# A pair-product kernel: W in one buffer, chunks aligned at their ends, one buffer for the transposed x

## The chip, the cores, the metric

The kernel runs on one core of a Trainium2 chip. The metric is the device time of one execution in microseconds; a quoted time is the median of a kernel's fast runs. TensorE (PE) does the matmuls, VectorE (DVE) the multiplications, ScalarE (ACT) copies out of PSUM and issues loads, SyncE (SP) issues the stores and W's loads, and 16 DMA engines move the data.

## The reference

For every row b of x (4096 rows, 32 fields of 64 numbers) and every pair of fields i < j, the output is `(x[b, i] @ W[pair]) * x[b, j]`, with one 64 x 64 matrix for each of the 496 pairs:

```python
i_idx, j_idx = np.triu_indices(32, k=1)
vdotw = einsum('bpd,pde->bpe', x[:, i_idx, :], W)   # x: 4096 x 32 x 64, W: 496 x 64 x 64
out = (vdotw * x[:, j_idx, :]).reshape(4096, -1)    # 4096 x 31744 float32 = 520 MB
```

## The kernel before

There are 32 tiles of 128 rows. Field i needs one matrix product whose right side is (31 - i) * 64 columns wide: all its matrices side by side. Two neighbouring fields make a "pair" p = 0 to 15 (fields 2p and 2p + 1); the even one uses partitions 0 to 63 of PE, the odd one 64 to 127. The odd field has 64 columns less. Pairs are cut in chunks of at most 512 columns a field. PE writes a chunk of both fields to two PSUM banks, and one DVE instruction multiplies both with x into an output ring in SBUF. Four stores a tile empty the ring.

```python
STORES = [[0, 1], [2, 3], [4, 5, 6], [7, 8, 9, 10, 11, 12, 13, 14, 15]]   # pairs of each store
PREFETCH_AT = [5, 6]
RING = 28160                                       # columns; a tile makes 31744
...
for p in range(NPR):                               # W: sixteen buffers, sixteen loads
    wp = const.tile([P, width[2 * p]], F32, tag=f"w{p}", name=f"w{p}")
    nc.sync.dma_start(out=wp, in_=w[:, woff[p] : woff[p] + width[2 * p]])
...
if t + 1 < NT and p in PREFETCH_AT:                # the next tile's x, transposed into a second buffer
    ...
    transpose_x(xTs[t + 1], t + 1, xs[t + 1], PREFETCH_AT.index(p))
for c0 in range(0, width[2 * p], CHUNK):           # chunks counted from the fields' starts
    n = [max(0, min(CHUNK, width[2 * p + h] - c0)) for h in range(2)]
    ...                                            # one matmul a field
    o = [off[2 * p + h] - o0 + c0 for h in range(2)]
    xj = [(2 * p + h + 1) * D + c0 for h in range(2)]
    if n[1] > half - BANK and o[1] + n[0] <= store_w[s]:
        nc.vector.tensor_tensor(                   # both fields, n[0] columns each
            runs(osb, o[0], o[1], n[0]), runs(pm, 0, half, n[0]),
            runs(xt, xj[0], xj[1], n[0]), ALU.mult)
    else:
        ...                                        # one instruction a field
nc.sync.dma_start(out=out[ts(t, P), o0 : o0 + store_w[s]], in_=osb)
```

In the last chunk of a pair the odd field has 64 columns less, but the joint instruction writes n[0] columns for both, so it writes 64 columns of rubbish past the odd field's end, where the next pair begins. The next pair's first instruction overwrites them.

Of the kernel before, what the change touches and what calls it, by code (L numbers as in the profile page):

```python
# [1 line left out]

# [6 lines left out]

F32 = mybir.dt.float32  # L10
ALU = mybir.AluOpType

P = 128
BANK = 512
BANKS = 8
CHUNK = BANK

STORES = [[0, 1], [2, 3], [4, 5, 6], [7, 8, 9, 10, 11, 12, 13, 14, 15]]
PREFETCH_AT = [5, 6]
RING = 28160  # L20


@with_exitstack
def pair_bilinear_kernel(
    ctx: ExitStack,
    tc: tile.TileContext,
    x: bass.AP,
    w: bass.AP,
    out: bass.AP,
    F: int,  # L30
    D: int,
):




















    nc = tc.nc
    B = x.shape[0]
    NT = B // P
    NPR = F // 2

    width = [(F - 1 - i) * D for i in range(F)]
    off = [sum(width[:i]) for i in range(F)]
    woff = [sum(width[0 : 2 * p : 2]) for p in range(NPR)]  # L60
    store_w = [sum(width[2 * p] + width[2 * p + 1] for p in g) for g in STORES]

    const = ctx.enter_context(tc.tile_pool(name="const", bufs=1))
    xtpool = ctx.enter_context(tc.tile_pool(name="xT", bufs=2))
    psum = ctx.enter_context(tc.tile_pool(name="ps", bufs=1, space=bass.MemoryType.PSUM))

    ident = const.tile([P, P], F32, tag="ident", name="ident")
    make_identity(nc, ident)

    def runs(tl, a, b, n):  # L70

        ap = tl[:, a : a + n]
        return bass.AP(ap.tensor, ap.offset, [list(ap.ap[0]), [b - a, 2], list(ap.ap[1])])


    xbuf = [const.tile([P, (F + 1) * D], F32, tag=f"x{b}", name=f"x{b}") for b in range(2)]
    for xb in xbuf:
        nc.gpsimd.memset(xb[:, F * D :], 0.0)  # L78

    def load_x(t):  # L80
        xt = xbuf[t % 2]
        nc.scalar.dma_start(out=xt[:, : F * D], in_=x[ts(t, P), :])
        return xt

    pring = psum.tile([P, BANKS * BANK], F32, tag="pring", name="pring")
    bank = 0

    def take_banks(n):

        nonlocal bank  # L90
        if bank + n > BANKS:
            bank = 0
        got = pring[:, bank * BANK : (bank + n) * BANK]
        bank = (bank + n) % BANKS
        return got

    def transpose_x(xT, t, xt, g):

        n = 2 * BANK // P
        pt = take_banks(2)  # L100
        for c in range(n):
            nc.tensor.transpose(pt[:, ts(c, P)], xt[:, ts(n * g + c, P)], ident)  # L102
        nc.scalar.copy(xT[:, ts(g, 2 * BANK)], pt)  # L103

    def new_xT(t):
        return xtpool.tile([P, NPR * P], F32, tag="xT", name=f"xT_{t}")

    ring = const.tile([P, RING], F32, tag="ring", name="ring")
    at = 0
    xs = {0: load_x(0)}  # L110

    w_sb = []
    for p in range(NPR):
        wp = const.tile([P, width[2 * p]], F32, tag=f"w{p}", name=f"w{p}")
        nc.sync.dma_start(out=wp, in_=w[:, woff[p] : woff[p] + width[2 * p]])
        w_sb.append(wp)

    xTs = {0: new_xT(0)}
    for g in range(2):
        transpose_x(xTs[0], 0, xs[0], g)  # L120

    for t in range(NT):
        xt, xT = xs.pop(t), xTs.pop(t)
        if t + 1 < NT:
            xs[t + 1] = load_x(t + 1)
        for s, group in enumerate(STORES):
            if at + store_w[s] > RING:
                at = 0
            osb = ring[:, at : at + store_w[s]]
            at += store_w[s]  # L130
            o0 = off[2 * group[0]]
            for p in group:
                if t + 1 < NT and p in PREFETCH_AT:
                    if t + 1 not in xTs:
                        xTs[t + 1] = new_xT(t + 1)
                    transpose_x(xTs[t + 1], t + 1, xs[t + 1], PREFETCH_AT.index(p))
                for c0 in range(0, width[2 * p], CHUNK):
                    n = [max(0, min(CHUNK, width[2 * p + h] - c0)) for h in range(2)]
                    half = -(-n[0] // BANK) * BANK
                    pm = take_banks(2 * half // BANK)  # L140
                    for b0 in range(0, n[0], BANK):
                        b1 = min(b0 + BANK, n[0])
                        for h in range(2):
                            if b0 < n[h]:
                                nc.tensor.matmul(  # L145
                                    pm[:, h * half + b0 : h * half + b1],
                                    xT[h * D : (h + 1) * D, ts(p, P)],
                                    w_sb[p][h * D : (h + 1) * D, c0 + b0 : c0 + b1],
                                    start=True,
                                    stop=True,  # L150
                                )
                    o = [off[2 * p + h] - o0 + c0 for h in range(2)]
                    xj = [(2 * p + h + 1) * D + c0 for h in range(2)]
                    if n[1] > half - BANK and o[1] + n[0] <= store_w[s]:
                        nc.vector.tensor_tensor(  # L155
                            runs(osb, o[0], o[1], n[0]),
                            runs(pm, 0, half, n[0]),
                            runs(xt, xj[0], xj[1], n[0]),
                            ALU.mult,
                        )  # L160
                    else:
                        for h in range(2):
                            if n[h]:
                                nc.vector.tensor_tensor(  # L164
                                    osb[:, o[h] : o[h] + n[h]],
                                    pm[:, h * half : h * half + n[h]],
                                    xt[:, xj[h] : xj[h] + n[h]],
                                    ALU.mult,
                                )
            nc.sync.dma_start(out=out[ts(t, P), o0 : o0 + store_w[s]], in_=osb)  # L170


# [33 lines left out]
```

## Time and profile before

| | before |
|---|---|
| time | 1337.95 us (1337.75 to 1338.13, 6 runs) |
| bytes moved | 562.9 MB: 520.1 written, 41.9 read, the rest instructions |
| busy: PE, DVE, ACT | 86%, 90%, 5% of the span |
| DMA engines | at nine tenths or more in 39 of 40 slices |
| DVE waits for stores | 68 us in 35 waits |

### The profile page before, as it was taken

The page shows a single profiled execution, that of the slowest core. Times are in us where ns is not written, and L with a number is a line of the kernel's source. Part 1 is how long each engine was busy: PE and PEld are TensorE (multiplying, and loading weights), DVE is VectorE, ACT ScalarE, POOL GpSimd, SP SyncE. Part 2 cuts the span into 40 slices and gives each one's busy share as a digit, 9 for nine tenths or more (in the row PEclk, how much of TensorE's full clock was granted, in tenths as well). Part 3 has the DMA queues.
Part 4 walks back from the last instruction along what each step waited for, and adds up shares of the span by engine and source line. Part 5 has one row for each costly group of instructions (what it writes and reads, how often), then busy time and mean ns, then how long its engine had stood idle before and what let it go on. Part 6 is the DMA issues. An engine that isn't in the chain of part 4 may idle for free. (4 is left out here: it accounts for less than half of the span.)

```text
span 1335.8 us, 13084 instructions
## 1 busy us (share of the span) xinstructions
PE 1154.1 (86%) x5376; PEld 529.9 (40%) x5376; DVE 1199.1 (90%) x1344; ACT 66.1 (5%) x65; POOL 0.9 (0%) x8
## 2 busy tenths in 40 slices
PE   7898898988888889898888898898988888888883
PEld 3343343433343444344334444343443333333331
DVE  5999898999899999899999899989988989999994
ACT  1000000000000000000000000000000000000000
POOL 0000000000000000000000000000000000000000
PEclk9999999899999999999999999999999999999997
DMA  9999999999999999999999999999999999999998
GB/s 392 435 426 431 436 408 434 415 426 431 419 417 425 428 429 416 418 424 420 424 436 419 418 421 426 424 426 421 418 430 414 426 423 413 424 427 430 418 420 370
DMA packets 25403, 562.88 MB, mean 421 GB/s; under 512 B 2944, under 2 KB 3328, under 8 KB 4864
## 3 DMA queue, kind: packets, MB, share of 16 engines
q1 hardware_dynamic: 20736, 528.49, 92.6%
q10 hardware_dynamic: 4608, 33.56, 6.0%
q8 instruction: 42, 0.69, 0.2%
q14 instruction: 17, 0.14, 0.0%
HBM read 41.94 MB, written 520.09 MB: 421 GB/s over the span
## 5 line engine op out<-in xcount | busy, mean ns | idle before, releaser
L155 DVE TENSOR_TENSOR ring<-pring,x 128x1024 f32<-128x1024 f32 (+3 forms) x1088 | 1154.2, 1107 | 116.9 <-DMA out_dram<-ring 68.0
L145 PE MATMUL pring<-w,xT 64*128 64x512 f32 (+4 forms) x4864 | 1087.8, 563 | 132.3 <-DVE ring L155 127.9
L145 PEld LDWEIGHTS pring<-w,xT 64*128 64x128 f32 x4864 | 472.9, 192 | 721.4 <-DVE ring L155 611.7
L103 ACT COPY xT<-pring 128x1024 f32<-128x1024 f32 x64 | 64.8, 1012 | 1197.1 <-PE pring L102 1197.1
L102 PE MATMUL pring<-ident,x 128*128 128x128 f32 x512 | 71.5, 285 | 30.7 <-DMA x<-in_x_dram 30.3
L102 PEld LDWEIGHTS pring<-ident,x 128*128 128x128 f32 x512 | 57.0, 144 | 65.6 <-issue 65.6
L164 DVE TENSOR_TENSOR ring<-pring,x 128x64 f32<-128x64 f32 (+4 forms) x256 | 70.9, 297 | 3.3
L103 ACT ACT_TABLE_LOAD x1 | 1.3, 1283 | 1.7 <-PEq L198 1.7
masks.py:199 POOL TENSOR_SCALAR_AFFINE_SELECT ident<-ident 128x128 f32<-128x128 f32 x1 | 0.3, 292 | 0.0
L78 POOL MEMSET x<- 128x64 f32 x2 | 0.2, 152 | 0.0
masks.py:197 POOL MEMSET ident<- 128x128 f32 x1 | 0.2, 204 | 0.3 <-POOLq L198 0.3
L198 POOL MEMSET const-bfloat16-1.0<- 128x1 bf16 x1 | 0.1, 101 | 0.0
L198 POOL MEMSET const-uint8-127<- 128x1 uint8 x1 | 0.1, 101 | 0.0
L198 POOL MEMSET const-float32-0.0<- 128x1 f32 x1 | 0.1, 98 | 0.2 <-issue 0.2
L198 POOL MEMSET const-float32-1.0<- 128x1 f32 x1 | 0.1, 98 | 0.0
## 6 DMA issues: line engine op xcount, KB each, us to landing
out_dram<-ring SPq DMA_DIRECT2D x32, 4896.0 KB, 18.6
out_dram<-ring SPq DMA_DIRECT2D x32, 3936.0 KB, 17.4
out_dram<-ring SPq DMA_DIRECT2D x32, 3776.0 KB, 19.0
out_dram<-ring SPq DMA_DIRECT2D x32, 3264.0 KB, 19.4
x<-in_x_dram ACTq DMA_DIRECT2D x32, 1024.0 KB, 17.8
w<-in_w_dram SPq DMA_DIRECT2D x1, 992.0 KB, 7.5
w<-in_w_dram SPq DMA_DIRECT2D x1, 928.0 KB, 11.8
w<-in_w_dram SPq DMA_DIRECT2D x1, 864.0 KB, 13.4
```

The source lines that it names most:

```text
L78: nc.gpsimd.memset(xb[:, F * D :], 0.0)
L102: nc.tensor.transpose(pt[:, ts(c, P)], xt[:, ts(n * g + c, P)], ident)
L103: nc.scalar.copy(xT[:, ts(g, 2 * BANK)], pt)
L145: nc.tensor.matmul(pm[:, h * half + b0 : h * half + b1], xT[h * D : (h + 1) * D, ts(p, P)], w_sb[p][h * D : (h + 1) * D, c0 + b0 : c0 + b1 ...
L155: nc.vector.tensor_tensor(runs(osb, o[0], o[1], n[0]), runs(pm, 0, half, n[0]), runs(xt, xj[0], xj[1], n[0]), ALU.mult,)
L164: nc.vector.tensor_tensor(osb[:, o[h] : o[h] + n[h]], pm[:, h * half : h * half + n[h]], xt[:, xj[h] : xj[h] + n[h]], ALU.mult,)
L198: nc = bacc.Bacc("TRN2", target_bir_lowering=False, num_devices=1)
```

## The change

The intent was less of everything: five loads of W instead of sixteen, one buffer for the transposed x instead of two, no padding of x. The chunks are now counted from the fields' ends. There both fields of a pair reach the same x columns, so one instruction can take the same columns of x for both (a step of 0), and the 64 overhanging columns fall in front of the odd field, on the end of the even one.

```diff
-PREFETCH_AT = [5, 6]
+LOADS = [[0], [1], [2, 3], [4, 5, 6], [7, 8, 9, 10, 11, 12, 13, 14, 15]]
+FIRST_HALF_AT, SECOND_HALF_AT = 9, 3
...
+    xT = const.tile([P, NPR * P], F32, tag="xT", name="xT")
...
+    w_sb = const.tile([P, sum(width[0::2])], F32, tag="w", name="w")
+    done = 0
+    for g in LOADS:
+        upto = woff[2 * g[-1]] + width[2 * g[-1]]
+        nc.sync.dma_start(out=w_sb[:, done:upto], in_=w[:, done:upto])
+        done = upto
...
+                if p == SECOND_HALF_AT:
+                    transpose_x(xt, 1)
+                if p == FIRST_HALF_AT and t + 1 < NT:
+                    transpose_x(xbuf[(t + 1) % 2], 0)
+                first = (width[2 * p] - 1) % BANK + 1
+                for c1 in range(first, width[2 * p] + 1, BANK):
+                    n = first if c1 == first else BANK
+                    c0 = c1 - n
...
+                    xj = xt[:, (2 * p + 1) * D + c0 : (2 * p + 1) * D + c1]
+                    o = [off[2 * p + h] - o0 + c0 - h * D for h in range(2)]
+                    if odd and (c0 or c1 < width[2 * p]):
                         nc.vector.tensor_tensor(
-                            runs(osb, o[0], o[1], n[0]),
-                            runs(pm, 0, half, n[0]),
-                            runs(xt, xj[0], xj[1], n[0]),
+                            runs(osb, o[0], o[1], n),
+                            runs(pm, 0, BANK, n),
+                            bass.AP(xj.tensor, xj.offset, [xj.ap[0], [0, 2], xj.ap[1]]),
                             ALU.mult,
                         )
```

The ring keeps its size, though 8 KB a partition of SBUF come free.

More of the change, by code (lines that the diff above doesn't have):

```diff
@@ L15 @@
 BANKS = 8
-CHUNK = BANK
 STORES = [[0, 1], [2, 3], [4, 5, 6], [7, 8, 9, 10, 11, 12, 13, 14, 15]]
-PREFETCH_AT = [5, 6]
+LOADS = [[0], [1], [2, 3], [4, 5, 6], [7, 8, 9, 10, 11, 12, 13, 14, 15]]
+FIRST_HALF_AT, SECOND_HALF_AT = 9, 3
 RING = 28160
@@ L53, in pair_bilinear_kernel @@
     nc = tc.nc
-    B = x.shape[0]
-    NT = B // P
+    NT = x.shape[0] // P
     NPR = F // 2
@@ L59, in pair_bilinear_kernel @@
     off = [sum(width[:i]) for i in range(F)]
-    woff = [sum(width[0 : 2 * p : 2]) for p in range(NPR)]
+    woff = [i % 2 * D + sum(width[i % 2 : i : 2]) for i in range(F)]
     store_w = [sum(width[2 * p] + width[2 * p + 1] for p in g) for g in STORES]
     const = ctx.enter_context(tc.tile_pool(name="const", bufs=1))
-    xtpool = ctx.enter_context(tc.tile_pool(name="xT", bufs=2))
     psum = ctx.enter_context(tc.tile_pool(name="ps", bufs=1, space=bass.MemoryType.PSUM))
@@ L73, in runs @@
         return bass.AP(ap.tensor, ap.offset, [list(ap.ap[0]), [b - a, 2], list(ap.ap[1])])
-    xbuf = [const.tile([P, (F + 1) * D], F32, tag=f"x{b}", name=f"x{b}") for b in range(2)]
-    for xb in xbuf:
-        nc.gpsimd.memset(xb[:, F * D :], 0.0)
+    xbuf = [const.tile([P, F * D], F32, tag=f"x{b}", name=f"x{b}") for b in range(2)]
     def load_x(t):
-        xt = xbuf[t % 2]
-        nc.scalar.dma_start(out=xt[:, : F * D], in_=x[ts(t, P), :])
-        return xt
+        nc.scalar.dma_start(out=xbuf[t % 2], in_=x[ts(t, P), :])
     pring = psum.tile([P, BANKS * BANK], F32, tag="pring", name="pring")
@@ L95, in take_banks, with transpose_x @@
         return got
-    def transpose_x(xT, t, xt, g):
+    xT = const.tile([P, NPR * P], F32, tag="xT", name="xT")
+    def transpose_x(xt, g):
         n = 2 * BANK // P
@@ L103, in transpose_x @@
         nc.scalar.copy(xT[:, ts(g, 2 * BANK)], pt)
-    def new_xT(t):
-        return xtpool.tile([P, NPR * P], F32, tag="xT", name=f"xT_{t}")
     ring = const.tile([P, RING], F32, tag="ring", name="ring")
     at = 0
-    xs = {0: load_x(0)}
-    w_sb = []
-    for p in range(NPR):
-        wp = const.tile([P, width[2 * p]], F32, tag=f"w{p}", name=f"w{p}")
-        nc.sync.dma_start(out=wp, in_=w[:, woff[p] : woff[p] + width[2 * p]])
-        w_sb.append(wp)
-    xTs = {0: new_xT(0)}
-    for g in range(2):
-        transpose_x(xTs[0], 0, xs[0], g)
+    load_x(0)
+    w_sb = const.tile([P, sum(width[0::2])], F32, tag="w", name="w")
[4 more added lines that the diff above has]
+        done = upto
+    transpose_x(xbuf[0], 0)
     for t in range(NT):
-        xt, xT = xs.pop(t), xTs.pop(t)
+        xt = xbuf[t % 2]
         if t + 1 < NT:
-            xs[t + 1] = load_x(t + 1)
+            load_x(t + 1)
         for s, group in enumerate(STORES):
@@ L132, in pair_bilinear_kernel @@
             for p in group:
-                if t + 1 < NT and p in PREFETCH_AT:
-                    if t + 1 not in xTs:
-                        xTs[t + 1] = new_xT(t + 1)
-                    transpose_x(xTs[t + 1], t + 1, xs[t + 1], PREFETCH_AT.index(p))
-                for c0 in range(0, width[2 * p], CHUNK):
-                    n = [max(0, min(CHUNK, width[2 * p + h] - c0)) for h in range(2)]
-                    half = -(-n[0] // BANK) * BANK
-                    pm = take_banks(2 * half // BANK)
-                    for b0 in range(0, n[0], BANK):
-                        b1 = min(b0 + BANK, n[0])
-                        for h in range(2):
-                            if b0 < n[h]:
-                                nc.tensor.matmul(
-                                    pm[:, h * half + b0 : h * half + b1],
-                                    xT[h * D : (h + 1) * D, ts(p, P)],
-                                    w_sb[p][h * D : (h + 1) * D, c0 + b0 : c0 + b1],
-                                    start=True,
-                                    stop=True,
-                                )
-                    o = [off[2 * p + h] - o0 + c0 for h in range(2)]
-                    xj = [(2 * p + h + 1) * D + c0 for h in range(2)]
-                    if n[1] > half - BANK and o[1] + n[0] <= store_w[s]:
@@ new lines, in pair_bilinear_kernel @@
+                if p == SECOND_HALF_AT:
[6 more added lines that the diff above has]
+                    c0 = c1 - n
+                    odd = width[2 * p + 1] and c1 > D
+                    pm = take_banks(2)
+                    for h in range(1 + bool(odd)):
+                        a = woff[2 * p + h] + c0 - h * D
+                        nc.tensor.matmul(
+                            pm[:, h * BANK : h * BANK + n],
+                            xT[h * D : (h + 1) * D, ts(p, P)],
+                            w_sb[h * D : (h + 1) * D, a : a + n],
+                            start=True,
+                            stop=True,
+                        )
+                    xj = xt[:, (2 * p + 1) * D + c0 : (2 * p + 1) * D + c1]
+                    o = [off[2 * p + h] - o0 + c0 - h * D for h in range(2)]
+                    if odd and (c0 or c1 < width[2 * p]):
@@ L161, in pair_bilinear_kernel @@
                     else:
-                        for h in range(2):
-                            if n[h]:
-                                nc.vector.tensor_tensor(
-                                    osb[:, o[h] : o[h] + n[h]],
-                                    pm[:, h * half : h * half + n[h]],
-                                    xt[:, xj[h] : xj[h] + n[h]],
-                                    ALU.mult,
-                                )
+                        for h in range(1 + bool(odd)):
+                            nc.vector.tensor_tensor(
+                                osb[:, o[h] + h * D : o[h] + n],
+                                pm[:, h * (BANK + D) : h * BANK + n],
+                                xj[:, h * D :],
+                                ALU.mult,
+                            )
             nc.sync.dma_start(out=out[ts(t, P), o0 : o0 + store_w[s]], in_=osb)
@@ L185 @@
     first = [sum(n[:i]) for i in range(F)]
-    halves = [
-        np.concatenate(
-            [
-                np.pad(wt[:, first[i] : first[i] + n[i]], ((0, 0), (0, h), (0, 0)))
-                for i in range(h, F, 2)
-            ],
-            axis=1,
-        )
-        for h in range(2)
-    ]
-    w = np.ascontiguousarray(np.stack(halves)).reshape(2 * D, -1)
+    w = np.zeros((2, D, sum(n[0::2]), D), wt.dtype)
+    for h in range(2):
+        of_h = [wt[:, first[i] : first[i] + n[i]] for i in range(h, F, 2)]
+        w[h, :, h : h + sum(n[h::2])] = np.concatenate(of_h, axis=1)
+    w = w.reshape(2 * D, -1)
     nc = bacc.Bacc("TRN2", target_bir_lowering=False, num_devices=1)
```

## The prediction

> **What bounds the kernel now.** I read the page first: the engines' totals, the slices, the DMA queues.
>
> ```profile
> span 1335.8 us, 13084 instructions
> ...
> PE 1154.1 (86%) x5376; PEld 529.9 (40%) x5376; DVE 1199.1 (90%) x1344; ACT 66.1 (5%) x65; POOL 0.9 (0%) x8
> ...
> DVE  5999898999899999899999899989988989999994
> ...
> DMA  9999999999999999999999999999999999999998
> GB/s 392 435 426 431 436 408 434 415 426 431 419 417 425 428 429 416 418 424 420 424 436 419 418 421 426 424 426 421 418 430 414 426 423 413 424 427 430 418 420 370
> ...
> q1 hardware_dynamic: 20736, 528.49, 92.6%
> q10 hardware_dynamic: 4608, 33.56, 6.0%
> ```
>
> DVE is 90% busy and PE 86%, but the DMA row is at nine tenths in every slice from the first to the last but one. The kernel writes 520 MB, which the change cannot shrink, and reads 42 MB. The chain of waits is of little use: it goes back only 3% of the span, all on DVE. So I asked who waits for whom:
>
> ```profile
> DVE ring L155 <- DMA out_dram<-ring: 68.0, 35, 3.0
> ...
> PE pring L102 <- DMA x<-in_x_dram: 30.3, 23, 8.5
> DVE ring L155 <- PE pring L145: 16.7, 7, 13.6
> ```
>
> The columns are total us, number of waits, the longest one. DVE waits 68 us for stores to clear the output ring, about once for each of the 32 tiles of 128 rows, and waits for PE hardly at all after its 13.6 us start. A ring full of stores means the stores are behind, not DVE. The timeline of DVE shows one such cycle (start, duration, what, and in brackets the idle time before it):
>
> ```profile
> 479.53 9.00 DVE L155 TENSOR_TENSOR ring<-pring,x 128x1024 f32<-128x1024 f32 x8 [2.44 <-DMA out_dram<-ring]
> ...
> 501.52 0.23 DVE L164 TENSOR_TENSOR ring<-pring,x 128x64 f32<-128x64 f32 x1
> 501.66 8.07 DVE L155 TENSOR_TENSOR ring<-pring,x 128x1024 f32<-128x1024 f32 x7
> ...
> 520.44 9.00 DVE L155 TENSOR_TENSOR ring<-pring,x 128x1024 f32<-128x1024 f32 x8 [2.40 <-DMA out_dram<-ring]
> ```
>
> A tile takes 520.44 - 479.53 = 40.9 us. DVE waits 2.4 us of it, at pair 4, for the previous tile's last and largest store; then it computes pairs 4 to 15 until 501.75 (501.52 + 0.23), when that tile's last store is issued. The median issue-to-landing time of these stores is 18.6 us, and 18.6 + 22.2 = 40.8: the loop closes. That alone would say that DVE's 22.2 us matter one for one. The packet records of the trace say otherwise. I sorted them onto 16 engines by letting each packet start where another ended. On 15 engines a 30,208-byte packet takes 1.119 us; on one it takes 1.149 us on average, and the 26,112- and 31,488-byte packets are also some 2% slower there. Summed over the kernel, that one engine is busy 1330.6 us of 1335.8, with 1.5 us of gaps after its first packet at 1.8 us and its last byte 1.3 us before the end. The other 15 are busy about 1312 us and idle about 17. Near 502 us the fifteen run dry for 0.6 us, until the new last store reaches them at 502.6; the slow one still has work until 505.6. Hence the bound: **one DMA engine that never stops**. DVE may be about 3 us later per tile, or any amount earlier, and the slow engine does not notice.
>
> **What the Trainium skill says.** "DMA: Bandwidth & Descriptors", section "Bandwidth", gives a fabric ceiling of 435 GB/s for the 16 engines together; the trace agrees: 421 GB/s over the whole span, up to 436 in a slice. 562.88 MB at 435 would be 1294 us, so no rearrangement of compute gets below that, 3.3% under today. The same page, "Latency and other measured facts", says that two of the 16 engines are usually slower in traces and suspects a descriptor ring that only GpSimd-issued DMAs have. The trace shows one slow engine with all DMAs issued from SP and ACT, so it agrees with the observation and not with that reason. "VectorE: DVE Perf Modes", section "The perf-mode tier table", has a two-tensor fp32 instruction with an operand in PSUM at one element a cycle, with no mode to gain or lose. The trace agrees: the 128x1024 multiply took 1217 ns and the 128x896 one 1079 ns, 1.08 ns per element between them (a cycle at the page's 0.96 GHz is 1.04 ns). I therefore expect nothing from x being read once for both fields: each field still streams its elements, merely from an address that repeats.
>
> **The change part by part.**
> (1) W in one buffer. W is the same 8.39 MB in five loads instead of 16. Its packets are one row each, and their durations lie on a line: 256 bytes 18 ns, 7,424 bytes 281 ns, so 0.0367 ns a byte plus about 8.6 ns a packet. Eleven fewer loads are 88 fewer packets on each engine (8 rows each): 88 x 8.6 ns = 0.76 us, plus 88/8 = 11 semaphore writes of 9 ns = 0.1 us. This lies on the bounding engine and at the front, where it shifts all that follows: -0.9 us. W now lands in coarser steps, which could starve PE: the loads finish at about 27.6 us whatever the cuts, and pair 7, the first of the last load, is reached near 38 us by the timeline. Pairs 2 and 3 (one load, done by an estimate of some 17 us from bytes at 424 GB/s) are reached at about 21 us. No wait.
> (2) Start. Only 8 of 16 transposes come before the first matmul. The timeline has PE transposing from 8.54 to 12.19 us and its first multiplying matmul at 12.12; the first copy of x's transpose ended at 11.53. So DVE starts 0.5 to 0.6 us sooner, and the first store would be issued at about 24.1 instead of 24.68. But the DMA engines are full of W until 27.6 us: worth nothing.
> (3) Chunk ends aligned. The matmul count is unchanged (4864 + 512), by the built program. DVE goes from 42 to 43 instructions a tile: pairs 1 and 6 become one instruction each instead of two, pairs 12 to 14 become two each instead of one.
>
> ```profile
> L155 DVE TENSOR_TENSOR ring<-pring,x 128x1024 f32<-128x1024 f32 x768 | 903.2, 1217 | 110.0 <-DMA out_dram<-ring 68.0 <-PE pring L145 16.7 <-PE pring L102 2.5
> ...
> L155 DVE TENSOR_TENSOR ring<-pring,x 128x896 f32<-128x896 f32 x128 | 138.1, 1079 | 0.0
> ...
> L155 DVE TENSOR_TENSOR ring<-pring,x 128x640 f32<-128x640 f32 x96 | 78.5, 818 | 3.7 <-DVE ring L155 0.5
> ...
> L155 DVE TENSOR_TENSOR ring<-pring,x 128x384 f32<-128x384 f32 x96 | 52.8, 550 | 3.2
> ...
> L164 DVE TENSOR_TENSOR ring<-pring,x 128x320 f32<-128x320 f32 x32 | 15.3, 480 | 0.0
> L164 DVE TENSOR_TENSOR ring<-pring,x 128x256 f32<-128x256 f32 x32 | 13.2, 411 | 0.0
> L164 DVE TENSOR_TENSOR ring<-pring,x 128x192 f32<-128x192 f32 x32 | 11.1, 347 | 0.0
> L164 DVE TENSOR_TENSOR ring<-pring,x 128x128 f32<-128x128 f32 x32 | 8.9, 279 | 0.0
> ```
>
> (Columns: count, then busy us, then mean ns of one.) Split forms grow by 67 ns per 64 elements, so 384 and 448 columns should cost about 547 and 614. Pair 1: 818 - (480 + 411) = -73. Pair 6: 550 - (347 + 279) = -76. Pairs 12 to 14: (614 + 547 + 480 + 411 + 347 + 279) - (1079 + 818 + 550) = +231. Sum +82 ns a tile, 2.6 us over 32; on the stretch from pair 4 to 15 it is +155 ns. Both are far inside the 3 us of slack: worth nothing. The overhanging columns that are computed and overwritten go from 10 to 9 a tile, in the same instructions' sizes as counted above.
> (4) One transposed-x buffer. Half of the transposes move to pair 9 of the tile before and half to pair 3. The 30.3 us that PE waits for x, 8.5 of it at the start and the rest at pair 5, because x lands near 521 us in the tile shown, vanish at pair 9, some 11 us later. DVE has three chunks buffered in PSUM then, and its wait for the transposes was 2.5 us in all. The overwritten half has long been read by PE, which is in order. Worth nothing. The freed SBUF is not given to the ring, which would be the only use of it that touches the DMA.
>
> Sum: -0.9 us. 1337.8 - 0.9 = 1336.9 us.
>
> **The rivals.**
> (a) DVE is the bound after all, through the loop 18.6 + 22.2. For it: the sum closes, and the fifteen engines' 0.6 us gap. Then +155 ns x 31 tiles = +4.8 us, 1342 us; or, if reading x twice from one place made DVE faster, up to 0.6 x 31 = 18 us less, 1319 us, where the fifteen engines would be full. Against it: the slow engine's 1.5 us of gaps in 1335.8.
> (b) The repeating read makes DVE slower. DVE has about 40.9 - 2.4 = 38.5 us of work a tile, so above 6% it would replace the DMA as the bound; 10% would give 42.4 us a tile, +1.5 x 31 = 46 us, 1384 us. Nothing in the trace speaks for it: joint reads with strides already run at the same rate as flat ones.
> (c) New waits of PE at pairs 3 and 9, or on the coarse W loads, stall DVE. A stall under 3 us a tile is hidden behind the slow engine; one at the start is hidden up to the 27.6 us at which W is done. 1337 us.
> (d) Another chip, with another slow engine or none. Without one, the fifteen's time would rule: about 1320 us for both kernels, no difference between them.
>
> **Range and chances.** The bytes are fixed and the bounding resource is full, so the spread is that of executions (0.3 us here) and of rival (a)'s small side, +5 or a few us less: 1331 to 1342. Faster by over 2% means below 1311, which needs the slow engine to lose 26 us of work: 0.01. Slower by over 2% needs rival (b): 0.02. Within 2%: 0.97.
>
> **What would show it.** DMA share again about 1 in all slices; the slow engine again without gaps; the tile period again 40.9 us; DVE's wait for stores still 60 to 75 us; W's packets about 19.6 us on an engine instead of 20.5; PE's wait for x about 8 us, all at the start; DVE's 128x1024 multiply at about 1217 ns. I am wrong if DVE's mean there rises by over 6%, if its waits for stores vanish, or if the period moves by more than 0.2 us.

## The result, and the profile after

| | before | after |
|---|---|---|
| time | 1337.95 us | 1338.02 us (1337.91 to 1338.11, 6 runs) |
| DVE waits for stores / for PE | 68.0 / 19.2 us | 101.6 / 22.8 us |
| PE waits for x | 30.3 us | 8.7 us |

The ratio is 1.0001 (95% interval 0.9988 to 1.0013). A ratio is the mean time of one kernel's fast runs over that of the other's of the same rounds, so not quite the ratio of the medians quoted. The change does nothing to the time.

The page of the kernel after (totals, slices, DMA queues; q1 carries W and the stores, q10 carries x):

```profile
span 1336.3 us, 13134 instructions
...
PE 1164.7 (87%) x5376; PEld 552.9 (41%) x5376; DVE 1183.0 (89%) x1376; ACT 66.1 (5%) x65; POOL 0.7 (0%) x6
...
DMA  9999999999999999999999999999999999999998
...
q1 hardware_dynamic: 19152, 528.49, 92.6%
q10 hardware_dynamic: 4608, 33.56, 6.0%
```

The DMA row and the bytes are as before; only the packets of q1 are fewer, 19,152 for 20,736. DVE has 32 instructions more and yet is 16 us less busy. Who waits for whom, after (total us, number, longest):

```profile
DVE ring L154 <- DMA out_dram<-ring: 101.6, 40, 4.1
DVE ring L154 <- PE pring L144: 22.8, 16, 13.6
...
PE pring L105 <- DMA x<-in_x_dram: 8.7, 1, 8.7
```

DVE waits 34 us longer for the stores: it became faster, and all of that turned into waiting. Of PE's waits for x only the first one, at the start, is left. The landing of the largest store (last column, median us from issue to landing), before and after:

```profile
out_dram<-ring SPq DMA_DIRECT2D x32, 4896.0 KB, 18.6
```

```profile
out_dram<-ring SPq DMA_DIRECT2D x32, 4896.0 KB, 19.5
```

It got longer as DVE's part got shorter. Since DVE waits for this landing in about every tile, landing and DVE's work roughly add up to the period whichever of them sets it. So "the sum closes" was no evidence for the prediction's rival (a). The timeline of DVE after, for the same tile as in the prediction:

```profile
479.66 6.81 DVE L154 TENSOR_TENSOR ring<-pring,x 128x896 f32<-128x896 f32 x7 [3.75 <-DMA out_dram<-ring]
...
499.12 2.40 DVE L162 TENSOR_TENSOR ring<-pring,x 128x448 f32<-128x448 f32 x7
501.44 12.46 DVE L154 TENSOR_TENSOR ring<-pring,x 128x896 f32<-128x896 f32 x12
...
520.61 6.81 DVE L154 TENSOR_TENSOR ring<-pring,x 128x896 f32<-128x896 f32 x7 [3.12 <-DMA out_dram<-ring]
```

The period is 520.61 - 479.66 = 40.95 us, as before. What changed is the wait at pair 4: 3.1 to 3.8 us in the tiles shown, instead of 2.4.

I sorted the trace's packet records onto 16 engines again (each packet starts where another ended, and each engine takes 8 packets of each store). The sorting can swap neighbours that end at the same time, but the engine that lags stands apart:

| run (its profiled execution, us) | span | slow engine busy | its gaps | the other fifteen busy |
|---|---|---|---|---|
| before | 1335.8 | 1330.6 | 1.5 | 1309 to 1316 |
| after | 1336.3 | 1331.5 | 1.1 | 1309 to 1315 |

A second, separate sorting gives the slow engine 1332.1 and 1332.5 us busy with 0.6 and 0.4 us of gaps, so these figures are good to about 2 us. It finds one slow engine of the 16 in the traces of all kernels here: about 1.00 us (median) for a packet of 26,112 bytes, where the others take 0.97.

### The profile page after: what moved, and what is told of

Its sections match the earlier page's. It is cut to its first block, busy times and chain, and to the rows that moved or that the text cites. A ratio compares the mean times of both kernels' runs of the same rounds, so it can differ in the third digit from the quotient of the medians.

```text
span 1336.3 us, 13134 instructions
## 1 busy us (share of the span) xinstructions
PE 1164.7 (87%) x5376; PEld 552.9 (41%) x5376; DVE 1183.0 (89%) x1376; ACT 66.1 (5%) x65; POOL 0.7 (0%) x6
## 3 DMA queue, kind: packets, MB, share of 16 engines
q1 hardware_dynamic: 19152, 528.49, 92.6%
## 4 chain that ended last, share of the span: by engine, by line
DMA 45%; DVE 36%; PE 9%; issue 8%; DVEq 0%; ACT 0%
DMA out_dram<-ring 45%; DVE ring L154 30%; PE pring L144 9%; DVE ring L162 5%; DMA x<-in_x_dram 1%; DVEq L154 0%; PE pring L105 0%; ACT xT L106 0%; DVEq L193 0%
## 5 line engine op out<-in xcount | busy, mean ns | idle before, releaser
L144 PE MATMUL pring<-w,xT 64*128 64x512 f32 (+4 forms) x4864 | 1102.6, 568 | 143.3 <-DVE ring L154 131.8
L154 DVE TENSOR_TENSOR ring<-pring,x 128x1024 f32<-128x1024 f32 (+3 forms) x1056 | 1104.6, 1107 | 135.3 <-DMA out_dram<-ring 101.6
L144 PEld LDWEIGHTS pring<-w,xT 64*128 64x128 f32 x4864 | 497.3, 194 | 706.5 <-DVE ring L154 508.4
L162 DVE TENSOR_TENSOR ring<-pring,x 128x64 f32<-128x64 f32 (+3 forms) x320 | 97.6, 355 | 0.3
## 6 DMA issues: line engine op xcount, KB each, us to landing
x<-in_x_dram ACTq DMA_DIRECT2D x32, 1024.0 KB, 18.1
```

What stands on the lines that cost most here:

```text
L144: nc.tensor.matmul(pm[:, h * BANK : h * BANK + n], xT[h * D : (h + 1) * D, ts(p, P)], w_sb[h * D : (h + 1) * D, a : a + n], start=True, st ...
L154: nc.vector.tensor_tensor(runs(osb, o[0], o[1], n), runs(pm, 0, BANK, n), bass.AP(xj.tensor, xj.offset, [xj.ap[0], [0, 2], xj.ap[1]]), ALU ...
L162: nc.vector.tensor_tensor(osb[:, o[h] + h * D : o[h] + n], pm[:, h * (BANK + D) : h * BANK + n], xj[:, h * D :], ALU.mult,)
```

## The experiments

Twelve kernels ran, in four calls, each on another chip (4, 5, 10 and 6); the kernel before ran in each call and took 1337.6 to 1338.0 us. Theory A is the prediction's: one DMA engine without gaps sets the time. Theory B, its rival, is the loop of a store's landing (18.6 us) and DVE's work behind it (22.2 us).

**DVE slower on purpose.** Two, then four of the 1024-wide multiplies are done twice, always behind the wait for the ring:

```diff
-                        nc.vector.tensor_tensor(...)
+                        for again in range(2 if p in [5, 7] and c1 == width[2 * p] else 1):   # again4: [5, 6, 7, 8]
+                            nc.vector.tensor_tensor(...)
```

> The changed kernel with two of its 128x1024 multiplies done twice in every tile, between pair 5 and pair 8, behind the wait for the ring (same result). Each repeat costs 1.22 us and a wait on DVE itself, about 1.3 us, so DVE has 2.6 us more a tile: about 37.2 + 2.6 = 39.8 us, still under the tile period of 40.95. Theory A (one DMA engine without gaps sets the period): no change, 1338 us within 2, and DVE's wait for stores falls from 101.6 us to some 20 to 30. Theory B (the loop store landing 18.6 us + DVE 22.2 us sets it): + 2.6 x 31 = +81 us, 1419 us.

> As the run with two, but four multiplies done twice in every tile: DVE has 5.3 us more, 37.2 + 5.3 = 42.5 us a tile, above the period. Theory A: DVE becomes the bound, + (42.5 - 40.95) x 31 = +48 us, about 1386 us, and DVE waits for hardly any store. Theory B: + 5.3 x 31 = +164 us, 1502 us.

Measured: 1340.34 us with two (1337.63 before in these rounds; ratio 1.0019, interval 1.0004 to 1.0034), and 1406.95 us with four. DVE's waits for stores, first with two, then with four:

```profile
DVE ring L155 <- DMA out_dram<-ring: 37.8, 28, 2.0
```

```profile
DVE ring L155 <- DMA out_dram<-ring: 25.6, 16, 2.5
```

Eighty microseconds of extra DVE work, by the estimate of 2.6 us a tile, cost under 3 us: the waits shrank from 101.6 to 37.8 us and absorbed most of it. Theory B, which wanted +81, is out. The 2.7 us aren't nothing; the slow engine's gaps rose from 1.1 to 4.0 us in this run, so the 3 us of slack a tile seem nearly used up. With four repeats DVE is the bound, as expected, but the time was 21 us above the expected 1386. The waits for stores did not go to nothing, as I had assumed, and the 25.6 us left are about that difference.

**Fewer bytes.** The last store of a tile leaves out its last 512 columns (wrong result):

```diff
-            nc.sync.dma_start(out=out[ts(t, P), o0 : o0 + store_w[s]], in_=osb)
+            keep = store_w[s] - (512 if s == 3 else 0)
+            nc.sync.dma_start(out=out[ts(t, P), o0 : o0 + keep], in_=osb[:, :keep])
```

> The changed kernel, wrong on purpose: the last store of every tile leaves out its last 512 columns; all else, DVE's work too, is the same. Each DMA engine moves 8 x 2,048 bytes less a tile, at 0.0368 ns a byte 0.60 us. If the DMA engines' work sets the time: - 0.60 x 32 = -19 us, 1319 us, although DVE, at 37.2 us a tile, does nothing less. If DVE or a wait that has nothing to do with bytes sets it: 1338 us.

Measured: 1319.05 us against 1337.67 before, ratio 0.9861. The time follows the bytes to the microsecond, and DVE's work didn't matter. It shows positively that the DMA engines' work sets the time; that one engine's counts, the runs that split x show below. The slow engine was busy 1311.4 us of a span of 1317.2, with 2.1 us of gaps.

**Only the aligned chunks.** W in sixteen loads (still into one buffer), two buffers for the transposed x, transposes at pairs 5 and 6:

```diff
+LOADS = [[p] for p in range(16)]
...
+PREFETCH_AT = [5, 6]
...
+    xTb = [const.tile([P, NPR * P], F32, tag=f"xT{b}", name=f"xT{b}") for b in range(2)]
...
+                if t + 1 < NT and p in PREFETCH_AT:
+                    transpose_x(xTb[(t + 1) % 2], xbuf[(t + 1) % 2], PREFETCH_AT.index(p))
```

> Only the aligned chunks of the change: W in sixteen loads (into one buffer) and two transposed-x buffers with both halves of the transposes at pairs 5 and 6, as before. If the aligned chunks are what made DVE faster (10 waits of DVE on its own last write became 3 a tile, 0.19 us each), DVE's wait for stores is about 100 us here too, against 68 before; if the moved transposes did it, it is near 68. Theory A: the time is 1338 us within 1 in both cases.

Measured: 1338.05 us (ratio 1.0004). DVE's waits in this kernel:

```profile
DVE ring L153 <- DMA out_dram<-ring: 80.6, 35, 3.6
...
DVE ring L153 <- PE pring L143: 34.7, 67, 13.1
DVE ring L153 <- PE pring L105: 6.1, 2, 3.7
```

The 80.6 us fall between the two numbers that I had set. The sum decides: 80.6 + 34.7 + 6.1 = 121 us of waiting, as in the full change (101.6 + 22.8 = 124) and unlike before (68.0 + 16.7 + 2.5 = 87). So the chunks made DVE faster. With the transposes at pairs 5 and 6, part of the time gained was spent waiting for PE; moving the transposes turned that into waiting for stores. Neither reaches the time.

**Is DVE's gain worth something where DVE is the bound?** The kernel before, with four multiplies done twice:

```diff
-                        nc.vector.tensor_tensor(...)
+                        for again in range(2 if p in [5, 6, 7, 8] and c0 == 0 else 1):
+                            nc.vector.tensor_tensor(...)
```

> The kernel before, with the first 1024-wide multiply of pairs 5, 6, 7 and 8 done twice in every tile (same result): DVE-bound like the changed kernel with four repeats, which took 1406.95 us. The changed chunks took 7 of 10 waits of DVE on its own last write away, 0.19 us each, and added 0.09 us of work: 1.2 us a tile. If that gain is real it appears where DVE is the bound: 1407 + 1.2 x 32 = about 1445 us here. If the chunks made DVE no faster, and its longer waits for stores came from something else, 1407 us.

Measured: 1429.2 us, so 22 us more than the changed kernel with four repeats (1406.95; the two ran on chips 5 and 4, where the kernel before took 1337.84 and 1337.63 us). The gain is real, 0.7 us a tile. It is smaller than the 1.2 us expected. Part of the difference is in the waits for stores, 18.1 us here and 25.6 there; without them it is (1428.0 - 18.1) - (1405.2 - 25.9) = 31 us of the two spans, 0.96 a tile. What the rest is, these runs do not tell: the repeats themselves change which instructions stand side by side.

**Sixteen loads into the one buffer.**

```diff
-LOADS = [[0], [1], [2, 3], [4, 5, 6], [7, 8, 9, 10, 11, 12, 13, 14, 15]]
+LOADS = [[p] for p in range(16)]
```

> The changed kernel with W still in one buffer, but loaded in sixteen pieces as before. The prediction gave the five loads a gain of 0.9 us through fewer packets. If that gain is there and something else in the change took it back: 1338.0 + 0.9 = 1338.9 us. If the five loads gain nothing, because the last, larger packets took longer (about 1.1 instead of 0.77 us at the end): 1338.0 us.

Measured: 1338.07 us (5 runs), the changed kernel's time. The five loads gain nothing.

**The freed memory given to the ring.**

```diff
-RING = 28160
+RING = 30208
```

> The changed kernel with the 8 KB a partition that the single transposed-x buffer freed given to the output ring (30,208 instead of 28,160 columns). If a full DMA engine is the bound, more room in front of it gains nothing: 1338 us within 2, only DVE's waits move. If the wait for ring space costs time, DVE's 102 us of waits for stores shrink and up to 0.6 x 31 = 18 us of idle time of fifteen DMA engines could go: down to 1320 us.

Measured: 1338.22 us, ratio 1.0004. DVE still waits 108 us for stores, and the slow engine has 0.8 us of gaps. More room in front of a full engine was worth nothing.

**Where is the slow engine?** The trace does not number the DMA engines. By the Trainium skill ("DMA: Bandwidth & Descriptors", section "Why a DMA increments its semaphore by 16 and not by 1") a load uses as many engines as the largest number up to 16 that divides its rows, the lowest-numbered ones. Each engine that took part ends its share with a small semaphore packet, an end mark. Their count agrees here: split in 120 and 8 rows, x's queue had 224 packets more, 7 a tile, and 15 + 8 is 7 more than 16. So one can give some engines more work.

```diff
-        nc.scalar.dma_start(out=xbuf[t % 2], in_=x[ts(t, P), :])
+        for r0, r1 in ((0, 120), (120, 128)):
+            nc.scalar.dma_start(out=xbuf[t % 2][r0:r1, :], in_=x[t * P + r0 : t * P + r1, :])
```

> The changed kernel with each load of x cut by rows in 120 and 8. By the number of rows the first should run on 15 of the 16 DMA engines, the last engine getting none, and the second should give one row more to each of eight engines. A row of x costs 0.31 us. Theory A, three cases by where the slow engine is. If it is the last one: it loses 8 x 0.31 = 2.5 us a tile, the others with 40.35 + 0.31 = 40.7 us a tile become the bound, 1338 - 0.25 x 31 = about 1330 us. If it is among the eight that get a ninth row: + 0.31 x 31 = +10 us, 1348 us. If it is one of the other seven: no change. Theory C (no single engine matters, the DMA engines' sum does): no change in any case, the bytes being the same.

Measured: 1358.16 us, +20.5. That is the case "among the first eight" in direction, but twice its size. Two side effects had not been in the expectation: DVE started 4.7 us later (x's two parts landed later, and W's loads were issued later), and x's packets took 0.325 instead of 0.311 us on average. The time alone can't tell these apart from the slow engine's ninth row. The trace can: the slow engine's packets follow each other without a gap, and in the 26 tiles in which this chain can be followed (chip 4) it took nine packets of x and two end marks, where in the changed kernel it took eight and one (28 tiles). So it is among the first eight. Next came an extra load of few rows:

```diff
+        nc.scalar.dma_start(out=spare, in_=x[t * P : t * P + 7, :])        # rows8: 8
...
+                        if p == NPR - 1:
+                            nc.vector.tensor_tensor(osb[:7, o[0] : o[0] + n], pm[:7, :n], spare[:, (F - 1) * D :], ALU.mult)
```

> The changed kernel with 7 rows of x loaded once more in every tile into a spare buffer (used in one more multiply of 64 columns, same result). By the number of rows this load should run on the first 7 of 16 DMA engines, one packet of 8,192 bytes, 0.31 us, on each. If the slow engine is among the first 7: + 0.31 x 32 = +10 us, 1348 us. If it is the eighth, as the split of x (+20 us) and the Trainium skill's remark on two slow engines together suggest: no change, 1338 us within 2, since the seven have 0.6 us a tile to spare.

> As the run with 7 rows, with 8: one row more, and one engine more, the eighth. If the slow engine is one of the first eight, as the split of x says: + 0.31 x 32 = +10 us, 1348 us, and if it is the eighth this one row is the whole difference between the two runs. If no single engine matters, both runs cost the same, 57 or 65 KB of 17.3 MB a tile, 0.4%: +5 us each.

Measured: 1352.40 and 1352.72 us, no difference between them. By its times alone the pair failed as a test, because the extra multiply at a tile's end also changed an order. It held the largest store back, and x's load, which did not wait for it, was issued 0.24 us ahead of that store (505.69 and 505.93 us in the tile that I looked at), where in the changed kernel the store comes first (501.55 us, x's load 501.56). The packets of x then took 0.415 us on average instead of 0.311. But not on all engines, as the next expectation has it: by the second sorting 0.34 us on the slow engine and over 0.4 on the others, which have time to spare.

The traces settle what the times do not. With seven rows (chip 5), the slow engine took nine packets of x and two end marks in 23 tiles, and in the last tile, where the spare rows are all that is loaded, it took one of the seven packets. So it is among the first seven and is not the eighth, which is also why the eighth row cost nothing. Its ninth packet accounts for about 10 us of the 14.6 (0.31 x 32); its somewhat longer packets of x are of the right size for the rest. What the order alone costs stays open. The reverse was tried next, x's load held back by pair 0 of the tile:

```diff
-        if t + 1 < NT:
-            load_x(t + 1)
+        if t == 0:
+            load_x(1)
...
+                if p == 1 and 0 < t < NT - 1:
+                    nc.scalar.copy(xbuf[(t + 1) % 2][:, :1], osb[:, width[0] - 1 : width[0]])
+                    load_x(t + 1)
```

> The changed kernel with each load of x held back until DVE has done pair 0 of the tile, about 5 us later, so that it doesn't start together with the tile's largest store (a one-column copy on ScalarE orders it; same result). The runs with 7 and 8 more rows of x had x's load 0.24 us ahead of the store, and 8,192-byte packets of 0.41 us on average instead of 0.31, on all engines: +14 us. If the order of the two matters that much, holding x back should take something off: the first 39,168-byte packets are 1.77 instead of 1.45 us, 0.3 us a tile, up to -10 us, 1328 us. If those 0.3 us lie on the fifteen engines that have time to spare, and not on the slow one: 1338 us within 2.

Measured: 1338.99 us, ratio 1.0009: nothing gained. In the changed kernel the longer first packets are on the fifteen engines with time to spare: 1.69 us there and 1.48 on the slow one, by the second sorting. Holding x back did not remove them either, it moved them to later packets of the store: the 39,168-byte packets took 1.504 us on average, against 1.482. With x held back, the split could be tried again without the two side effects known so far:

```diff
-        nc.scalar.dma_start(out=xbuf[t % 2], in_=x[ts(t, P), :])
+        cuts = (0, P) if t < 2 else (0, 120, P)
+        for r0, r1 in zip(cuts, cuts[1:]):
+            nc.scalar.dma_start(out=xbuf[t % 2][r0:r1, :], in_=x[t * P + r0 : t * P + r1, :])
```

> The kernel with x held back, which took 1339.0 us, with its loads of x from the third tile on cut in 120 and 8 rows: the first split of x again, without its two side effects (a start 5 us later, and x's packets stretched by starting together with the store). Slow engine among the first eight: one row of x more, 0.31 us a tile x 30 = +9 us, 1348 us. Among the next seven: no change, 1339 us. The last: 0.25 us a tile less, about 1331 us. If no single engine matters: no change.

Measured: 1353.93 us (chip 6), 15 us above the run without the split (chip 10). Same bytes, same DVE work, and 1% slower: the sum of bytes over the engines isn't what counts. The slow engine was busy 1346.3 us with 2.3 us of gaps; the other fifteen had 13 to 22 us of gaps. The trace shows nine packets of x on the slow engine in the 23 tiles that can be followed, so it is one of the first eight here too. The size is again over the +9 expected, 0.5 us a tile for one packet of 0.31 us, and the split had a side effect after all: the 30,208-byte packets took 1.150 us on average instead of 1.121. On the slow engine they and the 39,168-byte ones each took some 0.01 us more, 0.2 us a tile for sixteen packets, which is about the missing part. That the second DMA lengthens them is my guess; no run isolates it.

No version beats both kernels. To do so, one would have to take bytes off the slow engine alone. By the page's rule a load that leaves it out must run on fewer, lower-numbered engines, at most six; which of the first seven the slow engine is stays open.

## Why the prediction was right, and where it wasn't

The time was forecast at 1336.9 us and came out at 1338.02; what carried the forecast was the bound, and that held. Its one summand, -0.9 us, was wrong, and too small to show.

- **The bound: one DMA engine that never stops.** Right. The period of a tile is unchanged, the slow engine has 1.1 us of gaps after, the run with fewer bytes moved by the 19 us expected of it, and one packet more a tile on the slow engine, with the same bytes in all, cost 15 us. (The prediction's 1294 us, from the skill's 435 GB/s, is an estimate; no run came near it.) The slack of "about 3 us" a tile for DVE held as well: 2.6 us more cost only 2.7 us in all.
- **(1) "-0.9 us" for W's packets.** Wrong. The line through packet durations (8.6 ns a packet, 0.0367 ns a byte) was right for most of them: the 20,736-byte packets took 0.77 us, as it says. But from about 25 us on, most of the last quarter of them took 0.8 to 1.5 us, so W's packets took 20.9 us an engine instead of 21.3 on average, about half of the saving. On the slow engine they took 20.6 us instead of 20.7, and W was done there at 27.6 us in both kernels; but so near the start the sorting tells the engines apart poorly, and these last figures are uncertain. The first store had been issued at 23.13 us and came behind them; before, the last packets were of 256 to 2,304 bytes and kept to their line. The run with sixteen loads, 1338.07 us, shows that the five gain nothing. Why the large ones stretch at the end was not tested.
- **(2) The earlier start.** Right in effect: the first store was issued at 23.13 instead of 24.68 us, earlier than the 24.1 foreseen, and it was worth nothing.
- **(3) DVE's instructions: "+82 ns a tile", "DVE's wait for stores still 60 to 75 us".** The durations were right: 448 and 384 columns took 615 and 548 ns (614 and 547 foreseen), and 1024 columns still 1217 ns with x read twice from one place.

```profile
L154 DVE TENSOR_TENSOR ring<-pring,x 128x1024 f32<-128x1024 f32 x768 | 902.5, 1217 | 17.9 <-PE pring L144 6.6 <-DMA out_dram<-ring 0.3
...
L162 DVE TENSOR_TENSOR ring<-pring,x 128x448 f32<-128x448 f32 x32 | 19.7, 615 | 0.0
L162 DVE TENSOR_TENSOR ring<-pring,x 128x384 f32<-128x384 f32 x32 | 17.5, 548 | 0.0
```

  But DVE's pace isn't the sum of durations, and the wait became 101.6 us. The step that failed was "The overhanging columns [...] go from 10 to 9 a tile, in the same instructions' sizes as counted above". It counted the overhanging columns and not who must wait for them. Before, the overhang lies on the first columns of the next pair, so the very next DVE instruction waits until it is written: in the trace it starts 0.104 us (median) after its predecessor's end, where a free one starts 0.084 us before it. That is 0.19 us, ten times a tile. After, the overhang lies on the end of the pair's own even field, and in the wide pairs one or two other chunks lie between it and the instruction that corrects it. Nine instructions a tile still wait for an earlier write of DVE, but only three of them lose time, those of pairs 8 to 10, which have two chunks and so none between. The run with only the aligned chunks loses time at the same three places. 7 x 0.19 = 1.3 us a tile are saved, less 0.08: about 1.2, of which the waits for stores show (101.6 - 68.0) / 32 = 1.05. Here also lie DVE's 16 us less of busy time with more instructions: seven more a tile no longer wait and overlap their predecessor by 0.084 us, 7 x 0.084 x 32 = 19 us, less the 2.6 us of added work. This is the one real gain in the change, and it is off the path.
- **(4) One transposed-x buffer.** Right: PE's wait for x is 8.7 us, all at the start; the time is not touched.
- **Rivals.** (a) fell with the run with two repeats. (b) did not come: 1217 ns. (c) came in small and was hidden: DVE waits 22.8 us for PE instead of 19.2, 13.6 of it at the start in both. (d) did not come: there is one slow engine in the traces from all four chips.

## What to carry to other kernels

When several resources are near full, look for the one without gaps, and look at it one unit at a time: here the mean over 16 DMA engines hid the one that set the time. A faster engine in front of it only waits longer, as the 34 us did. When instructions overlap what they write, count who has to wait for the overlap: putting it where the correction comes a few instructions later was worth more than any instruction that was removed.

## What the Trainium skill lacked or had wrong

- "VectorE: DVE Perf Modes", section "The DRAIN you can't avoid", measured that semaphores between eight copies cost nothing extra, and has the next instruction wait for the empty pipe; it adds that one that is not held starts earlier, without a number. Here such a wait did cost something: a multiply that waited for its direct predecessor's write started 0.104 us after that one's end, and one without such a wait 0.084 us before: 0.19 us.
- "DMA: Bandwidth & Descriptors", section "Latency and other measured facts", names the engines 7 and 15 as usually slower and suspects a cause that only DMAs issued from GpSimd have. Here one engine is slow with none of those: 1.149 instead of 1.119 us for 30,208 bytes, 18 us over the kernel, and it sets the time. By the nine packets of x that it took in the run with seven spare rows it is among the first seven on that chip, so neither 7 nor 15 if the row counts the core's engines from 0, in the order in which loads take them.
- The same page has no number for the order of a load and a large store issued together: with x's load 0.24 us ahead of the store, its 8,192-byte packets took 0.415 instead of 0.311 us on average, but on the slow engine only 0.34. Nor has it that late packets of a large load can stretch: 0.8 to 1.5 us instead of 0.77 for 20,736 bytes, when a store had been issued behind them (the cause was not tested).
